# A mixture-of-experts combine: the last slot's rows by one-hot products instead of gathered rows

## The chip, the cores and the metric

The kernel runs on one core of a Trainium2 chip. The metric is the device time of one execution in microseconds (us). The engines are TensorE (PE in the profile; its weight loads are PEld), VectorE (DVE), ScalarE (ACT), GpSimd (POOL) and SyncE (SP). SP issues most DMAs; indirect DMAs are issued by POOL. Each engine works through its own queue in order.

## The reference

Four images of 384 channels by 32 x 32 (1024 tokens each) pass two layers:

```
x = x + scan_block(norm(x))                       selective scan, four directions
t = tokens(x);  t = t + moe(layernorm(t))         4 experts, 2 per token
x = x + attention(norm(x))                        8 heads of 64, q = k = v
t = tokens(x);  t = t + ffn(layernorm(t))
```

The part that matters here is `moe`: a gate gives each token a softmax over four experts, the best two are kept and their weights made to sum to one, each expert is `gelu(x @ w1 + b1) @ w2 + b2` with 384 -> 1536 -> 384, and a token's output is the weighted sum of its two experts' outputs. All is in 32-bit floats.

## The kernel before

The scan is the first loop: batch by batch, in four directions, in blocks of 128 partitions by 512 positions. POOL makes the products (L440, L468), ACT the exponentials (L449), DVE the recurrences (L454) and products (L461), PE the sums (L475). SP feeds it with loads (dtr, L424; bcs, L350). Everything behind the scan of a batch is its "tail": routing, experts, combine, attention and the feed-forward layer. The tail of batch b is written down after the scan of batch b+1, and a scheduler merges all instructions into one fixed order per engine by priorities and a model of times; the combine and some other parts have a raised priority (`high_priority(offset=FORWARD)`). So the tails of batches 0 to 2 lie among the scan's instructions, and that of batch 3 stands alone at the end.

The tail, with the names that the change touches:

- `clear` (L594) writes zeros to the array `rows` of one batch in DRAM, 19 DMAs of 128 rows on SP's queue, from a tile of zeros repeated three times per row.
- `spread` (L631) turns x to token order, stores the tokens, and normalizes them (L680). `places` (L697) computes on DVE, for each token and each of its two choices k, a row number `pos`, so that rows of one expert lie together. Then 64 indirect DMAs in all (16 per batch, L685) scatter the normalized tokens into `rows`.
- `experts` (L882) works through `rows` in NSLOT = 11 slots: eight of 256 rows, then three of 128. A slot's expert is read from a register; its weights come in eight tiles of tag "kw" (w1 in four, w2 in four), loaded by SP. `gather(s)` loads a slot's rows (tile xs) and transposes them on PE (L936) to xc. The products are h_ps (L954) and y_ps (L975); DVE adds the bias (L979), and the slot's outputs go to the array `made` in DRAM (L982; for the last slot on ACT's queue, else on SP's).
- `combine` (L986) loads the tokens, lets POOL make two diagonal matrices of gate weights (diag, L996), and then fetches the 2 x 1024 expert outputs by 16 indirect DMAs (L1005) from `made` into eight tiles got (tag "kw" as well). For each 128 tokens, `add` multiplies diag with got on PE (L1012) and adds the result to the tokens on DVE (L1015).
- `prologue` (L1024) takes the mean and variance of the new tokens (L1037, L1038), normalizes them on ACT and transposes them on PE, in two halves. `attention` (L1058) and `last_layers` (L1158) follow.

Tiles of one tag share a number of buffers: before the last batch 8 for "kw" and 5 for "k4" (slot rows, slot outputs, diag, and others); in the last batch 10 and 4. A PSUM bank of tag "p" is one of 3 in these parts.

An overflow test at the end (L518) takes the maximum of all attention sums, which are kept for all four batches.

Of the kernel before, what the change touches and what calls it, by code (L numbers as in the profile page):

```python
# [9 lines left out]
F32 = mybir.dt.float32  # L10
# [7 lines left out]
P = 128  # L18
# [25 lines left out]
NFULL = TOP * L // SLOT  # L44
NHALF = (NROW - NFULL * SLOT) // P
NSLOT = NFULL + NHALF

HEADS = 8
HD = 64
# [66 lines left out]
class Body:  # L116
# [367 lines left out]
    def open_tail(self, ctx):  # L484

        nc, tc, a = self.nc, self.tc, self.a
        self.dram = ctx.enter_context(tc.tile_pool(name="t_dram", bufs=1, space=DRAM))
        self.x2 = [
            self.dram.tile([L, D], F32, tag=f"x2_{b}", name=f"x2_{b}") for b in range(B)
        ]  # L490

        self.sums = self.const.tile(
            [P, B, HEADS // 2, MB * 2, NH], F32, tag="sums", name="sums"
        )
        return Room(tc, ctx, "t", NARROW)

    def tail_batch(self, b, x1, room):
# [7 lines left out]

    def first_layer(self, b, room):

        self.experts(b, self.slots, room)
        with self.tc.high_priority(offset=FORWARD):
            xt, xn, add = self.combine(b, *self.place, room)  # L510
            return self.prologue(xt, xn, room, add)

    def second_layer(self, b, xc, room, between):
        att = self.attention(xc, self.sums[:, b], room)
        with self.tc.high_priority(offset=FORWARD):
            self.last_layers(b, att, room, between if b < 2 else ())

    def overflow(self, room):  # L518

        nc = self.nc  # L520
        flag = self.const.tile([1, 1], I32, tag="flag", name="flag")
        top = room.tile([P, 1], "top", "top")
        nc.vector.tensor_reduce(
            top, self.sums.rearrange("p b t m i -> p (b t m i)"), AX.X, ALU.max
        )
# [21 lines left out]
    def moe_consts(self, room):  # L547
        nc, a, wp = self.nc, self.a, self.const


        turn = wp.tile([P, DC, P + NE], F32, tag="turn", name="turn")
        wg = turn[:, :, P:]
        nc.sync.dma_start(out=wg, in_=a["wg"].rearrange("(c p) e -> p c e", p=P))
        for c in range(DC):
            nc.vector.tensor_copy(turn[:, c, :P], self.ident)
        ps = room.bank("p", "wg_ps")
        for c in range(DC):
            nc.tensor.matmul(ps[:, :NE], self.ones, wg[:, c, :], start=(c == 0), stop=(c == DC - 1))
# [24 lines left out]
        self.slot_at = count("slot_at", [NSLOT], [[1, NSLOT]])  # L583


        size = NROW
        self.zero = wp.tile([P, P], F32, tag="zero", name="zero")
        nc.gpsimd.memset(self.zero, 0.0)
        self.rows, self.made = [], []
        for b in range(B):  # L590
            self.rows.append(self.dram.tile([size, D], F32, tag=f"rows{b}", name=f"rows{b}"))
            self.made.append(self.dram.tile([size, D], F32, tag=f"made{b}", name=f"made{b}"))

    def clear(self, b):  # L594

        nc = self.nc
        self.zeroed = []
        for at in range(0, NROW, P):
            ins = nc.sync.dma_start(
                out=self.rows[b][at : at + P, :].rearrange("p (c d) -> p c d", c=DC),  # L600
                in_=self.zero.unsqueeze(1).to_broadcast([P, DC, P]),
            ).ins
            self.depend(ins, self.under_way[b])
            self.zeroed.append(ins)
# [26 lines left out]
    def spread(self, b, x1, room):  # L631
# [39 lines left out]
        pos, gate, expert = self.places(sc, room)  # L671

        placed = []
        for m in range(MB):
            if m % 2 == 0:
                xt = room.tile([P, 2, D], "k4", "xt")
                nc.sync.dma_start(out=xt, in_=self.tokens(b)[:, m : m + 2, :])
            nc.scalar.activation(  # L680
                xt[:, m % 2, :], xt[:, m % 2, :], AF.Identity,
                bias=less[:, m : m + 1], scale=rstd[:, m : m + 1],
            )
# [11 lines left out]
        yield (pos, gate), (expert, placed)  # L695

    def places(self, sc, room):  # L697

# [137 lines left out]
        def later(n, before, name):  # L836
# [38 lines left out]
        weight = room.tile([P, TOP, nt], "g_weight", "g_weight")  # L875
        nc.vector.tensor_reduce(
            weight.rearrange("p k m -> p (k m)"),
            gates.rearrange("p k m e -> p (k m) e"), AX.X, ALU.add,
        )
        return pos, weight, expert  # L880

    def experts(self, b, routed, room):  # L882

# [36 lines left out]

        def gather(s):
            at, size = extent(s)
            xs = room.tile([P, size // P, D], "k4", "xs")
            queue = nc.scalar if s == 0 else nc.sync
            got = queue.dma_start(
                out=xs, in_=rows[at : at + size, :].rearrange("(t p) d -> p t d", p=P)
            ).ins
            for put in placed:
                self.depend(got, put)
            xc = room.tile([P, DC, size], "k4", "xc")  # L930
            for lo in range(0, DC, HF // size):
                ps = room.bank("p", "xc_ps").rearrange("p (r l) -> p r l", l=size)
                n = min(HF // size, DC - lo)
                for c in range(lo, lo + n):
                    for t in range(size // P):
# [4 lines left out]
                nc.vector.tensor_copy(xc[:, lo : lo + n, :], ps[:, :n, :])  # L940
            return xc

        weights, xc = fetch(0), gather(0)
        for s in range(NSLOT):
# [27 lines left out]
            for t in range(size // P):  # L972
# [9 lines left out]
            queue.dma_start(  # L982
                out=made[at : at + size, :].rearrange("(t p) d -> p t d", p=P), in_=y
            )

    def combine(self, b, pos, gate, room):  # L986


        nc = self.nc
# [12 lines left out]
        for m in range(MB):  # L1002
            got.append(room.tile([P, TOP, D], "kw", "got"))
            for k in range(TOP):
                nc.gpsimd.indirect_dma_start(  # L1005
                    out=got[m][:, k, :], out_offset=None, in_=self.made[b][:, :],
                    in_offset=bass.IndirectOffsetOnAxis(ap=pos[:, k, m : m + 1], axis=0),
                )
        def add(m):
            ps = room.bank("p", "w_ps")[:, :D]  # L1010
            for k in range(TOP):
# [513 lines left out]
```

## Time and profile before

| what | value |
|---|---|
| median of 3 runs | 4249.24 us (4240.75 to 4253.25) |
| the profiled execution | 4230.72 us; span from first to last instruction 4228.9 us |
| busy: PE, DVE, ACT, POOL | 3363 (80%), 2846 (67%), 2506 (59%), 3020 us (71%) |
| mean granted TensorE clock | 0.873 of full speed |
| DMA | 693.7 MB, 410,387 packets, of which 51,088 under 512 bytes |
| clears of `rows` | 76 DMAs of 192 KB; the median issue takes 0.636 us of SP |
| indirect DMAs | 64 scatters, 64 gathers; 0.97 and 0.95 us of POOL each |
| gathers begin at (batches 0 to 3) | 1313.7, 2267.5, 3248.8, 3932.9 us |

Times in views of the trace are from the start of the span. "Idle before" is the time an engine stood before a group, with the instruction that released it behind an arrow. A busy share is an average, so it is read by stage: until about 3400 us the scan runs with the tails of batches 0 to 2 among it; from there to the end the rest of batch 2 and all of batch 3's tail remain.

### The profile page before, as it was taken

The numbers are of one execution on the slowest core, as the hardware profiler recorded it, in microseconds if no ns is written. First come the engines' busy times: TensorE is split into PE (matmuls) and PEld (weight loads), VectorE is DVE, ScalarE is ACT, GpSimd is POOL, SyncE is SP. The second block draws the span as 40 slices with busy tenths as digits, with TensorE's granted clock in tenths as the row PEclk, the third lists the DMA queues.
The fourth block names the chain that finished last, engine by engine and source line by source line (L and its number), as shares of the span: only waits on it lengthen the run. The fifth ranks groups of instructions, "written<-read, shape, count | busy, mean of one in ns | idle before, by whom it ended". The sixth has DMA issues, their size and how long they took to land.

```text
span 4228.9 us, 45721 instructions
## 1 busy us (share of the span) xinstructions
PE 3363.3 (80%) x13308; PEld 1581.4 (37%) x13308; DVE 2846.4 (67%) x4152; ACT 2505.9 (59%) x4494; POOL 3020.1 (71%) x1471
## 2 busy tenths in 40 slices
PE   6544545489897888789996888789996899999898
PEld 2111111155553223245553223245553235566323
DVE  5999997878887878788887777888886840010101
ACT  5555555556665776666665777676664763443353
POOL 5999997898988978789899878889897840000100
PEclk8666666589998999789997999789997899999999
DMA  5454464677886535667887434658887434255200
GB/s 138 125 135 123 117 174 109 187 218 218 242 249 176 153 106 147 198 178 230 251 247 220 130 100 133 200 166 242 227 250 225 117 107 143 86 174 209 64 16 31
DMA packets 410387, 693.70 MB, mean 164 GB/s; under 512 B 51088, under 2 KB 209680, under 8 KB 410128
## 3 DMA queue, kind: packets, MB, share of 16 engines
q1 hardware_dynamic: 399728, 662.71, 54.1%
q0 software_dynamic: 8192, 25.17, 1.8%
q10 hardware_dynamic: 2208, 2.82, 0.2%
q8 instruction: 107, 1.75, 0.2%
q14 instruction: 152, 1.25, 0.1%
HBM read 569.00 MB, written 121.50 MB: 163 GB/s over the span
## 4 chain that ended last, share of the span: by engine, by line
PE 37%; DVE 22%; ACT 11%; DMA 11%; POOL 9%; issue 7%; SPq 3%; DVEq 0%; POOLq 0%; ACTq 0%
PE y_ps L975 9%; PE h_ps L954 9%; DVE da L454 8%; DVE bx L454 7%; POOL bx L440 5%; DMA dtr<-dd 4%; ACT da L449 3%; PE s_ps L1099 3%; PE acc L475 3%; DVE bx L461 3%; PE o_acc L1145 3%; POOL bx L468 2%; DMA w<-in_w 2%; SPq L424 2%; DMA bcs<-both 1%
## 5 line engine op out<-in xcount | busy, mean ns | idle before, releaser
L440 POOL TENSOR_TENSOR bx<-dtr,bcs 128x1024 f32<-128x1024 f32 x768 | 1794.0, 2363 | 201.6 <-PE acc L475 92.4
L449 ACT ACTIVATE da<-dtr,nega 128x512 f32<-128x512 f32 x1536 | 1045.3, 690 | 898.3 <-DVE bx L461 540.9
L468 POOL TENSOR_TENSOR bx<-bx,bcs 128x1024 f32<-128x1024 f32 x384 | 905.1, 2362 | 133.3 <-DVE carry L465 60.5
L475 PE MATMUL acc<-bx,sel 128*32 128x512 f32 x3072 | 500.2, 697 | 294.0 <-POOL bx L468 256.8
L954 PE MATMUL h_ps<-xc,w 128*128 128x256 f32 (+1 forms) x3168 | 675.8, 370 | 71.0 <-DMA w<-in_w 40.0
L975 PE MATMUL y_ps<-w,hs 128*128 128x384 f32 x1824 | 634.4, 500 | 26.7 <-ACT hs L967 20.1
L954 PEld LDWEIGHTS h_ps<-xc,w 128*128 128x128 f32 x3168 | 561.0, 201 | 240.7 <-issue 120.2
L454 DVE TENSOR_TENSOR_SCAN bx<-da,carry,bx 128x512 f32<-128x512 f32 x384 | 473.5, 1270 | 112.9 <-ACT da L449 57.7
L454 DVE TENSOR_TENSOR_SCAN da<-da,carry,bx 128x512 f32<-128x512 f32 x384 | 477.3, 1275 | 60.9 <-ACT da L449 50.2
L454 DVE TENSOR_TENSOR_SCAN bx<-da,bx 128x512 f32<-128x512 f32 x384 | 453.5, 1211 | 90.4 <-ACT da L449 56.8
L461 DVE TENSOR_TENSOR bx<-da,bcs 128x512 f32<-128x512 f32 x768 | 511.0, 681 | 4.0
L454 DVE TENSOR_TENSOR_SCAN da<-da,bx 128x512 f32<-128x512 f32 x384 | 456.1, 1219 | 76.6 <-ACT da L449 64.8
L975 PEld LDWEIGHTS y_ps<-w,hs 128*128 128x128 f32 x1824 | 348.4, 195 | 306.2 <-issue 64.7
L1105 ACT ACTIVATE ex<-s_ps 128x512 f32<-128x512 f32 x512 | 300.8, 592 | 130.1 <-PE s_ps L1099 126.6
L1099 PE MATMUL s_ps<-w 64*128 64x512 f32 x1024 | 310.6, 664 | 61.6 <-ACT ex L1105 56.3
L962 ACT ACTIVATE hs<-h_ps,bb 128x256 f32<-128x256 f32 (+1 forms) x528 | 200.5, 441 | 212.4 <-PE h_ps L954 208.2
L996 POOL TENSOR_TENSOR diag<-ident,g_weight 128x1024 f32<-128x1024 f32 x8 | 15.0, 1896 | 424.3 <-PE xc_ps L936 410.6
L1145 PE MATMUL o_acc<-ex,vt 128*64 128x512 f32 x1024 | 284.7, 633 | 24.0 <-ACT ex L1105 16.8
L475 PEld LDWEIGHTS acc<-bx,sel 128*32 128x32 f32 x3072 | 75.8, 116 | 594.1 <-POOL bx L468 361.7
L979 DVE TENSOR_TENSOR y<-y_ps,bb 128x384 f32<-128x384 f32 x76 | 41.6, 547 | 230.9 <-PE y_ps L975 230.6
L1099 PEld LDWEIGHTS s_ps<-w 64*128 64x128 f32 x1024 | 83.8, 190 | 267.2 <-ACT ex L1105 219.0
L365 PE MATMUL dt_ps<-xd,wdt 108*128 108x512 f32 x192 | 123.1, 728 | 63.4 <-ACT mag L404 34.4
(222 smaller groups left out, 3613.0 us busy)
## 6 DMA issues: line engine op xcount, KB each, us to landing
w<-in_w SPq DMA_DIRECT2D x352, 576.0 KB
dtr<-dd SPq DMA_DIRECT2D x1536, 128.0 KB
bcs<-both SPq DMA_DIRECT2D x512, 128.0 KB
dd<-one_e SPq DMA_DIRECT2D x96, 256.0 KB
dd<-mag SPq DMA_DIRECT2D x96, 256.0 KB
rows<-zero SPq DMA_DIRECT2D x76, 192.0 KB
xt<-x SPq DMA_DIRECT2D x32, 384.0 KB
made<-y SPq DMA_DIRECT2D x32, 384.0 KB
```

Of the source, the lines that this page charges most:

```text
L440: pool = nc.gpsimd.tensor_mul(bx, dtr[q][1], bc[:, 0].unsqueeze(1).to_broadcast([P, 2, HF])).ins
L449: nc.scalar.activation(da, dtr[q][0][:, j, :], AF.Exp, scale=nega[:, col : col + 1])
L454: nc.vector.tensor_tensor_scan(run(h), run(da), run(bx[:, j, :]), 0.0 if first else hold, ALU.mult, ALU.add,)
L461: dve = nc.vector.tensor_mul(bx[:, j, :], h, cg).ins
L468: pool = nc.gpsimd.tensor_mul(bx, bx, cg.unsqueeze(1).to_broadcast([P, 2, HF])).ins
L475: nc.tensor.matmul(acc[lo : lo + DB, :], sel, out[q][:, j, :], start=(g == 0), stop=(g == NG - 1),)
L954: ins = nc.tensor.matmul(ps[:, r, :], w1[(f + r) // wf][:, c, (f + r) % wf * P : ((f + r) % wf + 1) * P], xc[:, c, :], start=(c == 0), sto ...
L962: done = nc.scalar.activation(hs[:, f + r, :], ps[:, r, :], AF.Gelu if last else AF.Identity, bias=bb[:, f + r : f + r + 1],).ins
L975: nc.tensor.matmul(out[:, :D], hs[:, f, t * P : (t + 1) * P], w2[f // wf][:, f % wf, :], start=(f == 0), stop=(f == FC - 1),)
L1099: ins = nc.tensor.matmul(ps, w[rows, j * P : (j + 1) * P], w[rows, halves(i)], start=True, stop=True).ins
L1105: done.append(nc.scalar.activation(ex[:, o, :], ps, AF.Exp, scale=HD**-0.5, accum_out=sums[:, t, 2 * j + o, i : i + 1],).ins)
L1145: ins = nc.tensor.matmul(out[cols, :], made[t][1][:, j, cols], ex[:, o, :], start=(j == 0), stop=(j == MB - 1),).ins
```

## The change

The last slot's outputs are no longer stored and gathered. Each row in `rows` is one number wider (W = D + 1 = 385) and carries its token's number, 1 to 1024 (0 in a cleared row). When the last slot's rows are loaded, DVE compares that number with the numbers of each group of 128 tokens and gets eight one-hot matrices (`own`, tag "k4"). In `combine`, PE multiplies each with the last slot's output y (in SBUF), and DVE adds the product, times the gate weight `near` of tokens that have a row there, to the tokens. The gathers read `made` without its last 128 rows: where a token's row is in the last slot, its gather reads row 0 and its weight is 0. The rows are cleared by DMAs in pieces of 77 numbers, the largest divisor of 385 up to 128. The attention sums get a tile per batch instead of one for all, and each batch leaves one column of maxima.

```diff
+STORED = NROW - P
+W = D + 1
+WC = max(w for w in range(1, P + 1) if W % w == 0)
...
+        self.number = count("number", [MB], [[P, MB]], base=1, channel=1)
+        self.column = count("column", [P], [[1, P]], base=1)
...
@@ clear
-                out=self.rows[b][at : at + P, :].rearrange("p (c d) -> p c d", c=DC),
-                in_=self.zero.unsqueeze(1).to_broadcast([P, DC, P]),
+                out=self.rows[b][at : at + P, :].rearrange("p (c d) -> p c d", d=WC),
+                in_=self.zero[:, :WC].unsqueeze(1).to_broadcast([P, W // WC, WC]),
...
@@ spread
-                xt = room.tile([P, 2, D], "k4", "xt")
-                nc.sync.dma_start(out=xt, in_=self.tokens(b)[:, m : m + 2, :])
+                xt = room.tile([P, 2, W], "k4", "xt")
+                nc.sync.dma_start(out=xt[:, :, :D], in_=self.tokens(b)[:, m : m + 2, :])
+                nc.scalar.copy(xt[:, :, D:], self.number[:, m : m + 2].unsqueeze(2))
...
@@ places
+        nc.vector.tensor_scalar(stored, place, float(STORED) - 0.5, None, op0=ALU.is_lt)
+        nc.vector.tensor_mul(place, place, stored)
+        nc.vector.tensor_copy(source, place)
+        nc.vector.tensor_mul(weight, both, stored)
+        nc.vector.tensor_sub(rest, both, weight)
+        nc.vector.tensor_reduce(near, rest.rearrange("p k m -> p m k"), AX.X, ALU.add)
...
@@ experts, gather(s)
+            if s == NSLOT - 1:
+                apart = room.tile([P, MB], "apart", "apart")
+                nc.vector.tensor_sub(apart, xs[:, 0, D:].to_broadcast([P, MB]), self.full)
+                own = room.tile([P, MB, P], "k4", "own")
+                for m in range(MB):
+                    nc.vector.tensor_scalar(
+                        own[:, m, :], self.column, apart[:, m : m + 1], None, op0=ALU.is_equal
+                    )
...
-            queue = nc.sync if s + 1 < NSLOT else nc.scalar
-            queue.dma_start(
-                out=made[at : at + size, :].rearrange("(t p) d -> p t d", p=P), in_=y
-            )
+            if s + 1 < NSLOT:
+                nc.sync.dma_start(
+                    out=made[at : at + size, :].rearrange("(t p) d -> p t d", p=P), in_=y
+                )
...
@@ combine, behind the 16 gathers
+        own, y = last
+        for m in range(MB):
+            ps = room.bank("p", "n_ps")[:, :D]
+            nc.tensor.matmul(ps, own[:, m, :], y[:, 0, :], start=True, stop=True)
+            nc.vector.scalar_tensor_tensor(
+                xt[:, m, :], ps, near[:, m : m + 1], xt[:, m, :], op0=ALU.mult, op1=ALU.add
+            )
...
@@ second_layer
+        sums = room.tile([P, HEADS // 2, MB * 2, NH], "sums", "sums")
+        att = self.attention(xc, sums, room)
+        nc.vector.tensor_reduce(
+            self.tops[:, b : b + 1], sums.rearrange("p t m i -> p (t m i)"), AX.X, ALU.max
+        )
```

More of the change, by code (lines that the diff above doesn't have):

```diff
@@ L490, in open_tail @@
         ]
-        self.sums = self.const.tile(
-            [P, B, HEADS // 2, MB * 2, NH], F32, tag="sums", name="sums"
-        )
+        self.tops = self.const.tile([P, B], F32, tag="tops", name="tops")
         return Room(tc, ctx, "t", NARROW)
@@ L506, in first_layer @@
     def first_layer(self, b, room):
-        self.experts(b, self.slots, room)
+        last = self.experts(b, self.slots, room)
         with self.tc.high_priority(offset=FORWARD):
-            xt, xn, add = self.combine(b, *self.place, room)
+            xt, xn, add = self.combine(b, *self.place, last, room)
             return self.prologue(xt, xn, room, add)
     def second_layer(self, b, xc, room, between):
-        att = self.attention(xc, self.sums[:, b], room)
+        sums = room.tile([P, HEADS // 2, MB * 2, NH], "sums", "sums")
+        att = self.attention(xc, sums, room)
+        nc = self.nc
+        nc.vector.tensor_reduce(
+            self.tops[:, b : b + 1], sums.rearrange("p t m i -> p (t m i)"), AX.X, ALU.max
+        )
         with self.tc.high_priority(offset=FORWARD):
@@ L522, in overflow @@
         top = room.tile([P, 1], "top", "top")
-        nc.vector.tensor_reduce(
-            top, self.sums.rearrange("p b t m i -> p (b t m i)"), AX.X, ALU.max
-        )
+        nc.vector.tensor_reduce(top, self.tops, AX.X, ALU.max)
         ps = room.bank("p", "top_ps")
@@ L590, in moe_consts @@
         for b in range(B):
-            self.rows.append(self.dram.tile([size, D], F32, tag=f"rows{b}", name=f"rows{b}"))
-            self.made.append(self.dram.tile([size, D], F32, tag=f"made{b}", name=f"made{b}"))
+            self.rows.append(self.dram.tile([size, W], F32, tag=f"rows{b}", name=f"rows{b}"))
+            self.made.append(self.dram.tile([STORED, D], F32, tag=f"made{b}", name=f"made{b}"))
     def clear(self, b):
@@ L670, in spread @@
         less = self.less_mean(mv[:, :, 0], rstd, room, "r_less")
-        pos, gate, expert = self.places(sc, room)
+        pos, expert, place = self.places(sc, room)
         placed = []
@@ L677, in spread @@
             if m % 2 == 0:
-                xt = room.tile([P, 2, D], "k4", "xt")
-                nc.sync.dma_start(out=xt, in_=self.tokens(b)[:, m : m + 2, :])
+                xt = room.tile([P, 2, W], "k4", "xt")
+                nc.sync.dma_start(out=xt[:, :, :D], in_=self.tokens(b)[:, m : m + 2, :])
+                nc.scalar.copy(xt[:, :, D:], self.number[:, m : m + 2].unsqueeze(2))
             nc.scalar.activation(
-                xt[:, m % 2, :], xt[:, m % 2, :], AF.Identity,
+                xt[:, m % 2, :D], xt[:, m % 2, :D], AF.Identity,
                 bias=less[:, m : m + 1], scale=rstd[:, m : m + 1],
@@ L694, in spread @@
                 placed.append(put)
-        yield (pos, gate), (expert, placed)
+        yield place, (expert, placed)
     def places(self, sc, room):
@@ L874, in places @@
         nc.vector.tensor_mul(gates, chosen, sc.unsqueeze(1).to_broadcast([P, TOP, nt, NE]))
-        weight = room.tile([P, TOP, nt], "g_weight", "g_weight")
+        both = small([P, TOP, nt])
         nc.vector.tensor_reduce(
-            weight.rearrange("p k m -> p (k m)"),
+            both.rearrange("p k m -> p (k m)"),
             gates.rearrange("p k m e -> p (k m) e"), AX.X, ALU.add,
         )
-        return pos, weight, expert
+        stored = room.tile([P, TOP, nt], "g_stored", "g_stored")
+        nc.vector.tensor_scalar(stored, place, float(STORED) - 0.5, None, op0=ALU.is_lt)
+        nc.vector.tensor_mul(place, place, stored)
+        source = room.sb.tile([P, TOP, nt], I32, tag="g_source", name="g_source", bufs=2)
+        nc.vector.tensor_copy(source, place)
+        weight = room.tile([P, TOP, nt], "g_weight", "g_weight")
+        nc.vector.tensor_mul(weight, both, stored)
+        rest = room.tile([P, TOP, nt], "g_rest", "g_rest")
+        nc.vector.tensor_sub(rest, both, weight)
+        near = room.tile([P, nt], "g_near", "g_near")
+        nc.vector.tensor_reduce(near, rest.rearrange("p k m -> p m k"), AX.X, ALU.add)
+        return pos, expert, (source, weight, near)
     def experts(self, b, routed, room):
@@ L922, in gather @@
             at, size = extent(s)
-            xs = room.tile([P, size // P, D], "k4", "xs")
+            xs = room.tile([P, size // P, W], "k4", "xs")
             queue = nc.scalar if s == 0 else nc.sync
@@ L940, in gather @@
                 nc.vector.tensor_copy(xc[:, lo : lo + n, :], ps[:, :n, :])
+            if s == NSLOT - 1:
[6 more added lines that the diff above has]
+                    )
+                self.own = own
             return xc
@@ L979, in experts, with combine @@
                 nc.vector.tensor_add(y[:, t, :], out[:, :D], bb[:, FC:])
-            queue = nc.sync if s + 1 < NSLOT else nc.scalar
-            queue.dma_start(
-                out=made[at : at + size, :].rearrange("(t p) d -> p t d", p=P), in_=y
-            )
-    def combine(self, b, pos, gate, room):
+            if s + 1 < NSLOT:
+                nc.sync.dma_start(
+                    out=made[at : at + size, :].rearrange("(t p) d -> p t d", p=P), in_=y
+                )
+        return self.own, y
+    def combine(self, b, pos, gate, near, last, room):
         nc = self.nc
```

## The prediction

> **What bounds the kernel now.** I read four views, in this order. First the page's slices of the span (one digit is the busy share of 105.7 us in tenths):
>
> ```profile
> PE   6544545489897888789996888789996899999898
> ...
> POOL 5999997898988978789899878889897840000100
> ```
>
> POOL is nearly full until slice 31; after it PE is full to the end. So the scan (on POOL, DVE and ACT) sets the time to about 3400 us and TensorE sets the rest, with the tail of batches 0 to 2 threaded through the scan. Second, the timeline around the last batch's combine (start, length, engine, then in brackets how long the engine had been idle and who released it):
>
> ```profile
> 3921.61 8.01 PE L975 MATMUL y_ps<-w,hs 128*128 128x384 f32 x24 [2.04 <-ACT hs L959]
> ...
> 3930.25 0.34 ACTq L982 DMA_DIRECT2D made<-y  x1
> 3932.91 1.01 POOL L1005 DMA_INDIRECT got<-made,g_pos  x1 [12.44 <-DMA made<-y]
> 3935.97 0.97 POOL L1005 DMA_INDIRECT got<-made,g_pos  x1 [2.06 <-issue]
> ...
> 3936.21 1.62 PE L1012 MATMUL w_ps<-got,diag 128*128 128x384 f32 x2 [6.59 <-DMA got<-made,g_pos]
> ```
>
> Here nothing else runs: the last slot's product ends at 3929.6, is stored, and only then do 16 gathers go out, 1.256 us apart. Third, busy time by stage around the same place in batch 1 (columns: length; PE, PEld, DVE, ACT, POOL busy; granted clock; DMA share; GB/s):
>
> ```profile
> 2235.00:2257.00 22.00, 19.96 (x114) 13.77 (x114) 14.48 (x16) 16.95 (x29) 19.65 (x11) 0.94 0.77 244
> 2257.00:2268.00 11.00, 2.14 (x11) 0.35 (x9) 10.86 (x13) 7.50 (x13) 10.85 (x6) 0.70 0.39 125
> 2268.00:2288.00 20.00, 14.94 (x46) 6.91 (x47) 6.28 (x15) 6.02 (x12) 15.42 (x17) 0.67 0.73 214
> 2288.00:2310.00 22.00, 7.79 (x27) 3.35 (x25) 18.86 (x30) 8.83 (x16) 20.29 (x10) 0.66 0.57 143
> ```
>
> PE is idle for 28 of the 53 us after the product (2257 to 2310), and in the 20 us of the gathers DVE and ACT stand at 30%, for POOL issues gathers and feeds them nothing. Fourth, the chain of waits where SP clears the next batch's rows:
>
> ```profile
> 3205.71 12.58 DMA rows<-zero
> ...
> 3224.49 0.64 SPq L599
> ...
> 3225.18 0.63 SPq L599
> ...
> 3230.12 3.61 DMA dtr<-dd
> ```
>
> The clear stands on the chain, and the scan's own loads (dtr) are queued behind it.
>
> **Part 1, the exposed combine of batch 3.** Before: the product ends at 3929.6 and the statistics of the first half of the tokens are done at 3948.98 (ACT's first instruction after them). After, the gathers no longer wait for the last slot's store. They need the store of the slot before (issued 3915.96; POOL is released by it at 3918.57) and diag (done 3920.5). With 2 us before the second (the 2.06 above) and 1.256 each, the eighth goes out at about 3931.3 and lands 3.2 later (median of the gathers), 3934.5. What is added lies on the path: eight one-hot products of two passes each. The nearest row is the slot's own product, 24 passes in 7.74 us, so 0.645 for one, 5.2 for eight. They run 3930.3 to 3935.5, and DVE's eight multiply-adds (0.552 each, from L1015, same shape, one bank) keep pace. Then four w_ps of 1.29 (the pace of L1015 in the second half, 3955.66 to 3959.53) end at 3940.7, and the last add, statistics and aggregate are 1.3: about 3942. That is 7 earlier; with the clock of 0.73 granted there (3930 to 3955; 0.97 in the 150 us before) the ten us of products become up to 14 and 3 remain. I take **-6**. Bounds: -12, the whole shift of the gathers (3932.9 to 3920.5), if the products hid too; +5 if the second diag came last (rival D). What is late next is TensorE itself: from here it is busy to the end.
>
> **Part 2, the same in batches 0 to 2.** TensorE's 5.2 us of one-hot products have cover: it is idle for 15 us in 1290 to 1334, 28 in 2257 to 2310 and 22 in 3208 to 3254. Without that cover they would cost 5.2 each. The 64 gathers stay (rows that are not stored read row 0), so POOL's 20.1 us per batch stay too, and the scan stands still for them wherever they are. What can be won is that they lie beside the last slot's products (8.0 to 10.9 us on PE) rather than behind them. Ends: 0, since POOL's sum is the same, and -20, if all of the block moves beside work. I take batch 3's figure, -6 each, for it is the same chain: **-18**.
>
> **Part 3, the rows are one number wider.** 385 elements have 77 as their largest divisor up to 128, so each of the 19 clears of a batch writes 640 pieces of 308 bytes where it wrote 384 of 512. Now 19 clears take 12.86 us (1414), 13.33 (2314), and 14.4 for 17 of them at 3211, at a DMA share of 0.86 to 1.07. Ends: by bytes nothing; by pieces 640/384 x 0.64 us, so 0.43 more each and 8.2 per batch; and 4.6 per batch below nothing if SP's issue alone decided (wqkv, a load of 384 pieces of 512 bytes, is issued in 0.40). The engines are full in these stretches, so I take the pieces. The chain passes right behind the clears at 534 (POOL then waits 0.42 us for dtr), through those at 2314 and 3205, and not through that at 1414: three of four, **+24.6**. The DMA page of the Trainium skill ("DMA: Bandwidth & Descriptors", Specifications) speaks against this part: it says that transfers below 512 bytes miss line rate because the engine reads, modifies and writes. If by that rule the bytes cost twice, a clear would be 1.28 us, an estimate, and this term 36 in place of 24.6. The profile counts 51,088 packets under 512 bytes, but no large transfer of this kernel is made of them, so no row shows their price.
>
> **Part 4, VectorE and ScalarE.** Per batch DVE gains eight comparisons for the one-hot (128x128; between 0.19 for 128x32 at L737 and 0.414 for 128x384 at L1175, so about 0.25, 2.0 together), the eight multiply-adds (4.4) and seven small ones (0.17, 1.2): 7.6. In the slices of the combines DVE is 72 to 76% busy, and it is what hides them; without cover it would be 7.6 per batch. I take 1 for each of three batches, **+3**. The comparisons run before the last slot's product ends, with only that batch's scan behind them. The extra place arithmetic comes after the positions are cast, so the scatter does not wait for it in data. ACT's 16 copies of a number (0.17, as L541) are hidden behind the scatters' 1.27 us pace. The maxima of the sums (0.68 at 4132, long before the end) become four smaller ones, nothing. The scatter's 64 issues of 0.97 stay; one float more per row is nothing to them. The last slot's store leaves ACT's queue (0.34), nothing.
>
> **Sum**: -6 - 18 + 24.6 + 3 = +3.6 on the profiled execution, 4230.7 to 4234.3. That execution lies 18.5 below the median of the three runs (4249.2), so I carry the difference: 4253.
>
> **The rivals.** About 0.3%, 12.7 us, is what can be told from no change.
>
> *A, the forecast*: the terms cancel, 4240 to 4266.
>
> *B, the clears cost by bytes and the gathers lie well*: part 3 nothing, half of the 20.1 us beside the products in each batch: -6 - 30 + 3 = -33, **4216**. For it: PE's 15 to 28 idle us; DMA is only at 0.86 in two clears. Against: DMA at 1.07 in the last.
>
> *C, a new wait on POOL, slower*: the tiles that the gathers fill share eight buffers with the expert weights. In batches 0 to 2 the last slot's weights fill all eight: the first eight gathers wait for its h_ps products, the other eight for its y_ps products. A gather that waits in POOL's queue holds the scan's multiplications behind it, and DVE and ACT behind those. It decides once the y_ps product ends later than 17.6 us (14 gathers) after POOL reached the first. Price: the 12.4 us that POOL stood at its first gather in batch 3, with nothing behind; here three times with the scan behind: -6 + 36 + 24.6 + 3 = +58, **4307**. For it: POOL's queue is in order and 90% full. Against: in batches 0 to 2 it now waits at most 1.26 us at gathers.
>
> *D, it does not do what it says*: the tag k4 has four buffers in batch 3, and the one-hot holds one until its last product. If the second diag gets that one, it starts at 3935.5, ends at 3937.4, and the gathers, if queued behind it, begin 4.5 us later than now, and the statistics with them. With nothing won in the other batches: +5 + 24.6 + 3 = +33, **4282**. For it: in batch 3 the second diag already waits for a buffer, until 3918.57. Against: two other buffers come free before the one-hot's.
>
> **How the numbers follow.** A 0.36, B 0.30, C 0.18, D 0.16. A's upper end is past 4262, so 0.06 of it counts as slower: faster 0.30, same 0.30, slower 0.06 + 0.18 + 0.16 = 0.40. The range reaches from B to between D and C: 4213 to 4296; outside are the better half of B's spread (0.10) and C's worse half (0.09). A's own range is 4240 to 4266.
>
> **What would show it.** Part 1: the first gather of batch 3 starts before the last y_ps product ends, and the first half's statistics end 12 to 16 us behind that product, where it is 19.4 now. Part 2: no gather behind the last slot's product in batches 0 to 2, and the PE idle time there shrinks. Part 3: SP's 19 clears take 21 us (13 if bytes decide), and data packets under 512 bytes rise by 48,640. C would show as POOL waiting for PE at a gather; D as a diag released by a one-hot product. I am wrong if the order in which the engines' queues are written changes elsewhere too: any shift in the scan of more than 13 us outweighs all of this.

## The result and the profile after

| | before | after |
|---|---|---|
| median of 6 runs each | 4242.66 us (4240.75 to 4253.25) | 4359.54 us (4350.44 to 4365.40) |
| ratio, 95% interval | | 1.0267 (1.0252 to 1.0283) |
| span of the profiled execution | 4228.9 us | 4348.6 us |
| POOL idle behind dtr loads (line of the first scan product) | 80.1 us | 180.3 us |
| packets; under 512 bytes | 410,387; 51,088 | 429,268; 99,664 |
| the scan's last product on POOL ends at | 3412.9 us | 3516.5 us |
| from there to the end of the span | 816.0 us | 832.1 us |

The change costs 113 us by the ratio and 120 by the two profiled spans. The last two rows say where: 104 us are lost while the scan runs, 16 behind it. The slices of the span (a slice is now 108.7 us) show the same; POOL loses tenths in many slices of the scan, and still ends in slice 32:

```profile
PE   6445434489887688789987688879985799999899
...
POOL 5999977898888677879889768889885840000100
```

The largest loss is found by looking for what POOL waits for. This is the timeline of the changed kernel where SP clears batch 1's rows (start, length, engine, line, operation; in brackets the idle time before and who ended it), SP's queue first (the view opens behind the first of the 19 clears), then POOL:

```profile
1431.78 32.36 SPq L605 DMA_DIRECT2D rows<-zero  x18
1464.24 4.00 SPq L353 DMA_DIRECT2D bcs<-both  x4
1469.56 5.83 SPq L427 DMA_DIRECT2D dtr<-dd  x4
```

```profile
1445.66 2.36 POOL L471 TENSOR_TENSOR bx<-bx,bcs 128x1024 f32<-128x1024 f32 x1 [3.04 <-DVE carry L468]
1477.70 13.89 POOL L443 TENSOR_TENSOR bx<-dtr,bcs 128x1024 f32<-128x1024 f32 x6 [29.68 <-DMA dtr<-dd]
```

In the kernel before, the same clear on SP's queue was this line:

```profile
1413.94 12.86 SPq L599 DMA_DIRECT2D rows<-zero  x19
```

The clears now hold SP's queue for 33 us, the scan's loads stand behind them, and POOL stops for 29.7 us. It stops in the same way at all four clears: 25.3, 29.7, 22.8 and 27.0 us, **104.8 together**. SP's 19 issues of one clear took 12.9 to 13.3 us before (19.3 in batch 3, in two groups); they take 32.0, 33.0, 34.2 and 36.7 now. SP is held because the DMA engines are: here are 15 us from the first issue of batch 0's clear, where little else is under way. The columns are the window and its length, busy time of PE, PEld, DVE, ACT and POOL, the granted clock, the DMA share and GB/s. The kernel before:

```profile
534.07:549.07 15.00, 3.87 (x16) 0.40 (x16) 14.30 (x16) 6.67 (x10) 15.00 (x7) 0.51 0.86 259
```

The changed kernel, with the 15 us that follow:

```profile
529.78:544.78 15.00, 3.87 (x16) 0.40 (x16) 14.30 (x16) 6.67 (x10) 15.00 (x7) 0.50 1.24 105
544.78:559.78 15.00, 3.87 (x16) 0.40 (x16) 7.90 (x10) 4.07 (x6) 7.44 (x4) 0.50 1.38 100
```

The DMA engines are busier than before (1.24 to 1.38 against 0.86) and move 40% as much. More pieces alone, at the old price of a piece, would have left 384/640, 60%; so each piece takes longer as well.

Behind the scan, look first at the combine of batch 3, the one whose working the prediction shows. The timeline of the changed kernel (the lines between, 14 gathers among them, are left out):

```profile
4039.69 0.98 POOL L1035 DMA_INDIRECT got<-made,g_source  x1 [440.26 <-issue]
...
4042.32 8.01 PE L1004 MATMUL y_ps<-w,hs 128*128 128x384 f32 x24 [2.04 <-ACT hs L988]
...
4050.98 5.43 PE L1042 MATMUL n_ps<-y,own 128*128 128x384 f32 x16 [0.65 <-DVE y L1008]
...
4060.30 0.94 POOL L1035 DMA_INDIRECT got<-made,g_source  x1 [0.30 <-issue]
4061.26 3.76 POOL L1026 TENSOR_TENSOR diag<-ident,g_weight 128x1024 f32<-128x1024 f32 x2
...
4063.23 7.74 PE L1050 MATMUL w_ps<-got,diag 128*128 128x384 f32 x16 [6.82 <-POOL diag L1026]
...
4072.79 0.30 ACT L155 ACTIVATE rstd<-mv,eps 128x4 f32<-128x4 f32 x1 [28.18 <-DVE mv L1076]
```

The second diag and the first statistics in the kernel before:

```profile
3918.57 1.89 POOL L996 TENSOR_TENSOR diag<-ident,g_weight 128x1024 f32<-128x1024 f32 x1 [13.73 <-DMA made<-y]
...
3948.98 0.30 ACT L152 ACTIVATE rstd<-mv,eps 128x4 f32<-128x4 f32 x1 [25.09 <-DVE mv L1038]
```

The gathers do start 10.6 us before the last product ends (4050.3), and the one-hot products take 5.43 us. But the two diag products, which in the kernel before stood ahead of the gathers on POOL, now stand **behind all sixteen**, PE waits 6.82 us for them, and the first statistics are ready 22.5 us behind the product, where it was 19.4.

That gain is missed, but the 16 us lost behind the scan do not lie here: from the last product to the end of the span it is 298.3 us, against 299.3 before. They lie in front of it, between the scan's last product and the last product of batch 3's experts, where PE is busy for 495 of 517 us before and 511 of 534 now. What is left of batch 2's attention is worked off there. These views of that stretch count the products of attention scores (s_ps) alone, all of them of batch 2 (columns: busy time of PE, PEld, ACT with counts; clock, DMA share, GB/s). The kernel before, then the changed one:

```profile
3412.90:3929.60 516.70, 44.75 (x150) 11.91 (x148) 48.27 (x152) 0.98 0.44 149
```

```profile
3516.50:4050.30 533.80, 54.09 (x180) 14.50 (x180) 57.65 (x182) 0.97 0.44 147
```

Of a batch's 256 score products 180 are left when the scan ends, where it was 150, and the stretch is 17 us longer.

### The profile page after: what moved, and what is told of

It is laid out like the page before. It is cut to its first block, busy times and chain, and to the rows that moved or that the text cites. A ratio compares the mean times of both kernels' runs of the same rounds, so it can differ in the third digit from the quotient of the medians.

```text
span 4348.6 us, 45959 instructions
## 1 busy us (share of the span) xinstructions
PE 3377.8 (78%) x13372; PEld 1592.3 (37%) x13372; DVE 2870.9 (66%) x4250; ACT 2511.3 (58%) x4512; POOL 3020.7 (69%) x1473
## 2 busy tenths in 40 slices
DMA packets 429268, 693.04 MB, mean 159 GB/s; under 512 B 99664, under 2 KB 228560, under 8 KB 429008
## 3 DMA queue, kind: packets, MB, share of 16 engines
q14 instruction: 153, 1.25, 0.1%
## 5 line engine op out<-in xcount | busy, mean ns | idle before, releaser
L443 POOL TENSOR_TENSOR bx<-dtr,bcs 128x1024 f32<-128x1024 f32 x768 | 1794.3, 2366 | 287.2 <-DMA dtr<-dd 180.3
L1004 PE MATMUL y_ps<-w,hs 128*128 128x384 f32 x1824 | 644.5, 507 | 71.6 <-ACT hs L996 35.6
L1035 POOL DMA_INDIRECT got<-made,g_source x64 | 61.0, 953 | 460.3 <-issue 454.2
```

Of the source, the lines that this page charges most:

```text
L443: pool = nc.gpsimd.tensor_mul(bx, dtr[q][1], bc[:, 0].unsqueeze(1).to_broadcast([P, 2, HF])).ins
L1004: nc.tensor.matmul(out[:, :D], hs[:, f, t * P : (t + 1) * P], w2[f // wf][:, f % wf, :], start=(f == 0), stop=(f == FC - 1),)
```

## The experiments

Ratios are to runs of the kernel before that were taken on the same chip beside the kernel in question: 4272.09 us for experiments 1 to 4, 4247.64 for 5 and 7 to 9, 4248.79 for 6 and 10 to 12. Times of different chips are compared by these ratios. "Whole" below means that a piece starts and ends on a multiple of 32 bytes of the array, "cut" that it does not.

**Theories.** *Short pieces*: the clear in 308-byte pieces costs nearly all of it, because pieces under 512 bytes are dear. *Cut ends*: 308 is no multiple of the block that memory is written in, and that is what costs, not the length. *The rest*: the wider rows, the one-hot work or the order of the queues.

**1. The changed kernel, one piece of 1540 bytes a row.**

```diff
-                out=self.rows[b][at : at + P, :].rearrange("p (c d) -> p c d", d=WC),
-                in_=self.zero[:, :WC].unsqueeze(1).to_broadcast([P, W // WC, WC]),
+                out=self.rows[b][at : at + P, :],
+                in_=self.zero,
```

> The changed kernel, but each row is cleared in one piece of 1540 bytes (from a wider tile of zeros) instead of five of 308. Theory 1 (short pieces make the clears slow and the scan's loads wait behind them on SP): a batch's 19 clears fall from 32 to 37 us to 13 or less, the four waits of POOL for dtr behind them (25, 30, 23, 27 us) vanish, and the time falls by about 100, to 4245 to 4265. Theory 1b (it is not the length but the start off a 64-byte line, as the row pitch is 1540 bytes): clears stay above 25 us and the time above 4320. Theory 2 (gathers among the scan's products and the one-hot products hold up the scan): clears fall, but the time stays above 4310.

Measured: 4298.17 us, ratio 1.0061 (1.0038 to 1.0084). Of 2.67%, 2.1 are gone with the pieces alone: some 87 us, where about 100 was foretold. The clears of batches 0 to 2 took SP 10.7 to 12.0 us. So a start off the line does not by itself make a piece slow (theory 1b), for most rows of 1540 bytes start off it too; with short pieces it does, as run 3 shows.

**2. The kernel before, with the changed kernel's clear and nothing else.** The array is 385 numbers a row long and cleared whole in 308-byte pieces; rows stay 384 wide.

```diff
-                out=self.rows[b][at : at + P, :].rearrange("p (c d) -> p c d", c=DC),
-                in_=self.zero.unsqueeze(1).to_broadcast([P, DC, P]),
+                out=self.flat[b][at * W : (at + P) * W].rearrange("(p c d) -> p c d", p=P, d=WC),
+                in_=self.zero[:, :WC].unsqueeze(1).to_broadcast([P, W // WC, WC]),
```

> The kernel before, with nothing changed but the clears: the array has room for 385 numbers per row and is cleared whole in pieces of 308 bytes, 640 per DMA; rows themselves stay 384 wide. Theory 1: 19 clears take 32 to 37 us and the time rises by 80 to 115 over the kernel before, nearly all of the change's loss. Theory 2: it rises by less than 40.

Measured: 4382.94 us, ratio 1.0259 (1.0242 to 1.0276). The clear alone makes the loss: 111 us, with clears of 35.7 to 39.7 us on SP. In the page's group of the scan's first product the wait for dtr is 161.5 us (180.3 in the changed kernel, 80.1 in the kernel before):

```profile
L442 POOL TENSOR_TENSOR bx<-dtr,bcs 128x1024 f32<-128x1024 f32 x768 | 1792.5, 2360 | 296.7 <-DMA dtr<-dd 161.5
```

**3. Length against position.** The kernel before, each batch's clear in another kind of piece: 384 bytes, 256 bytes, 512 bytes moved by 4, 768 bytes.

```diff
+PIECE = (96, 64, 128, 192)
+SHIFT = (0, 0, 1, 0)
...
+                out=self.flat[b][SHIFT[b] + at * D : SHIFT[b] + (at + P) * D].rearrange(
+                    "(p c d) -> p c d", p=P, d=PIECE[b]
+                ),
```

> The kernel before as a probe: batch 0 clears its rows in pieces of 384 bytes, batch 1 in 256, batch 2 in 512 shifted by 4 bytes, batch 3 in 768. Read are the times of SP's 19 clears. If a piece has a fixed price when short (48 ns per engine, as the changed kernel's 1.94 us for 640 pieces gives): 1.55 us each for 384 bytes, 2.3 for 256. If the bytes count double below 512: 1.3 for both. If pieces cost the same as those of 512 bytes (27 ns): 0.85 and 1.28. The shifted ones stay at 0.64 if only length counts, and go above 1.2 if a start off the line has its own price; 768 bytes: 0.65 or less.

Measured: 4307.59 us (one run). The windows of 15 us from the first issue of batches 0 (384), 1 (256) and 2 (512 moved by 4), columns as above:

```profile
531.80:546.80 15.00, 3.87 (x16) 0.41 (x16) 14.30 (x16) 6.67 (x10) 15.00 (x7) 0.50 0.93 258
```

```profile
1421.97:1436.97 15.00, 11.37 (x58) 4.36 (x57) 14.77 (x27) 11.24 (x25) 13.08 (x7) 0.77 1.15 263
```

```profile
2337.58:2352.58 15.00, 13.28 (x51) 6.29 (x52) 12.72 (x13) 9.99 (x18) 8.92 (x5) 0.70 1.17 124
2352.58:2367.58 15.00, 5.90 (x26) 1.45 (x20) 3.12 (x5) 7.09 (x14) 3.20 (x2) 0.87 1.28 115
```

SP's 19 issues took 13.3, 13.4 and 23.1 us, so 0.70, 0.70 and 1.21 each. For the first two that is below the least that was foretold (0.85 and 1.28). Position decides. Pieces of 384 and even 256 bytes run at 258 and 263 GB/s, as the 512-byte pieces of the kernel before; pieces of **512 bytes that start 4 bytes off** run at 124. Length alone is refuted.

**4. The changed kernel, cleared flat in whole 512-byte pieces.**

```diff
+        flat = self.rows[b].rearrange("r d -> (r d)")
...
+                out=flat[lo : lo + step].rearrange("(p c d) -> p c d", p=P, d=P),
+                in_=self.zero.unsqueeze(1).to_broadcast([P, DC, P]),
```

> The changed kernel, its array cleared as one run of numbers in pieces of 512 bytes on 512-byte boundaries, as the kernel before does it (one more small DMA per batch for the rest). Theory 1 and 1b: clears of 13 us, time 4240 to 4265, the same as with one piece of 1540 bytes under theory 1, and 60 or more faster than it under 1b. What is left against the kernel before is the one-hot and the order of the queues: my sum without part 3 gave -21, theory 2 gives more than +60.

Measured: 4285.56 us, ratio 1.0036 (1.0021 to 1.0051). It cannot be told from run 1, and it lies between what my sum without part 3 gave (-21 us) and what theory 2 asked for (over +60): some 15 us of loss. Without the cut pieces the change is still not a gain; something else eats what parts 1 and 2 should bring.

**5. How large is the block.** As 3: batch 0 in 512-byte pieces moved by 64 bytes, batch 1 by 32, batch 2 by 16, batch 3 in 768-byte pieces moved by 4.

```diff
-PIECE = (96, 64, 128, 192)
-SHIFT = (0, 0, 1, 0)
+PIECE = (128, 128, 128, 192)
+SHIFT = (16, 8, 4, 1)
```

> The kernel before, its clear in pieces whose start is shifted by a constant: batch 0 in 512-byte pieces shifted by 64 bytes, batch 1 by 32 bytes, batch 2 by 16 bytes, batch 3 in 768-byte pieces shifted by 4 bytes. Theory "cut ends" (a piece whose ends do not fall on a block boundary costs more, whatever its length; 512-byte pieces shifted by 4 bytes took a DMA share of 1.29 at 118 GB/s, while 384 and 256 bytes unshifted took 0.94 to 1.09 at 257 to 271 GB/s): batch 0 about 13 us and 250 GB/s if blocks are 64 bytes, batch 1 the same only if blocks are 32 bytes, batch 2 slow in both cases, batch 3 slow but per byte about two thirds of the extra of a shifted 512-byte piece. Slow is a stretch of at least 20 us with a DMA share over 1.15 at under 160 GB/s. Theory "length" (only pieces under 512 bytes are dear): all four batches at 240 GB/s or more.

Measured: 4269.27 us (one run). Batches 0, 1 and 2:

```profile
529.55:544.55 15.00, 3.87 (x16) 0.40 (x16) 14.30 (x16) 6.67 (x10) 15.00 (x7) 0.50 1.07 252
```

```profile
1415.80:1430.80 15.00, 11.37 (x57) 4.44 (x56) 14.77 (x27) 11.25 (x25) 13.34 (x7) 0.77 1.09 261
```

```profile
2320.00:2335.00 15.00, 8.95 (x32) 3.39 (x30) 13.42 (x24) 11.54 (x22) 15.00 (x8) 0.97 1.16 122
```

Moved by 64 and by 32 bytes a piece runs at 252 and 261 GB/s, moved by 16 at 122. Of the moves tried, those by whole 32-byte blocks cost little (a mean of 34 ns for 27 in the trace's records of single pieces), and a piece that cuts a block is dear. Batch 3 lay among other loads (SP's issues took 26 us), and its rate could not be read.

**6. What a cut piece costs.** As 3, all moved by 4 bytes, in pieces of 768, 256, 384 and 512 bytes.

```diff
+PIECE = (192, 64, 96, 128)
+SHIFT = (1, 1, 1, 1)
```

> The kernel before, its clears shifted by 4 bytes in all batches, in pieces of 768, 256, 384 and 512 bytes. Measure: DMA-engine time in the 80 us from the first issue of the clear, where unshifted pieces took 49 to 55 us in batch 0, 37 to 45 in batch 1, 38 to 49 in batch 2. Theory "a price for each cut piece", 40 to 64 ns on its engine: 256 bytes (912 pieces an engine) take 36 us more or fill the 80 us, 384 bytes (608) 24 to 39 us more, 768 bytes (304) 12 to 19 us more. Rival "long pieces hide it": 768 bytes take at most 5 us more, as pieces of 1540 bytes did (49.6), and below some length each piece takes a fixed time whatever it carries. Under "length alone" 768 and 512 bytes would take nothing more.

Measured: 4389.36 us (one run). Batches 0 (768), 1 (256) and 2 (384); batch 3 again lay among other loads:

```profile
531.10:546.10 15.00, 3.87 (x16) 0.40 (x16) 14.30 (x16) 6.67 (x10) 15.00 (x7) 0.51 1.06 166
```

```profile
1425.60:1440.60 15.00, 11.37 (x59) 4.56 (x58) 14.77 (x28) 11.40 (x25) 13.49 (x6) 0.77 1.40 78
```

```profile
2370.70:2385.70 15.00, 11.81 (x50) 5.43 (x50) 12.81 (x13) 10.01 (x17) 10.93 (x6) 0.87 1.20 101
```

In time per piece on one of 16 engines (16 x bytes / rate; an estimate, since the windows hold a little other traffic), and behind it the mean of the pieces' own durations, of which the trace has one record each:

| piece, bytes | whole: GB/s, ns, mean record | cut: GB/s, ns, mean record |
|---|---|---|
| 256 | 263, 16, 18 | 78, 53, 95 |
| 308 | | 105, 47, 66 |
| 320 (run 7) | 229, 22, 26 | |
| 384 | 258, 24, 22 | 101, 61, 85 |
| 512 | 259, 32, 27 | 124, 66, 79 |
| 768 | record 36 (run 3, batch 3) | 166, 74, 88 |
| 1540 (run 1) | | 261, 94, 98 |

Whole pieces take time about by their bytes, down to 256. By the rate a cut piece takes 47 to 74 ns up to 768 bytes, and at 1540 the rate is that of whole 512-byte pieces. The records show more than the rates. Some cut pieces are as short as whole ones (20 ns for a quarter of those of 308 bytes), others take several times as long, and the mean lies 32 to 77 ns above the short ones, at 1540 bytes too (98 against 66; in the kernel before, half of all whole 1536-byte packets take 65 or less). So long pieces pay as well; it does not push their rate below that of whole 512-byte pieces. Neither of the simple forms on record holds, not by bytes and not one fixed addition. The engine time in the 80 us from the first issue was 57.3 us for the 768-byte pieces (50.2 in the kernel before), 7 more with 1.6 MB less of all traffic done, where the first form asked for 12 to 19; for 384 bytes it was about 39 more (24 to 39 foretold), and those of 256 bytes filled the 80 us, as foretold. One thing is not told apart: in every cut clear here a block that one piece cuts is also written by its neighbour, so the price may be that of a block written in part or of a block that two pieces share.

**7. The changed kernel with rows of 1600 bytes, cleared in pieces of 320.** The number stands 16 times in each row.

```diff
-W = D + 1
-WC = max(w for w in range(1, P + 1) if W % w == 0)
+W = D + 16
+WC = 80
```

> The changed kernel with rows of 400 values (1600 bytes; the token number stands 16 times in each) and the clear in pieces of 320 bytes, five a row, 640 a DMA for each engine's sixteenth 40, nothing else changed. Theory "cut ends": 320 bytes are a multiple of 64, so a clear costs as the aligned ones, 12 to 17 us a batch and 220 to 280 GB/s, and the ratio is 1.000 to 1.006. Theory "length": 320 bytes are as dear as 308, about 30 to 36 us a batch at 100 to 120 GB/s, ratio 1.022 to 1.030.

Measured: 4276.66 us, ratio 1.0063 (1.0038 to 1.0088), a hair above what cut ends had foretold (1.000 to 1.006) and far from the 1.022 of short pieces; SP's clears of batches 0 to 2 took 14.6 to 15.8 us. In the same place as above:

```profile
532.90:547.90 15.00, 3.87 (x16) 0.41 (x16) 14.30 (x15) 6.67 (x10) 15.00 (x8) 0.50 1.15 229
```

Twelve bytes more a piece, and the rate is 229 for 105.

**8. Wide rows alone.** The kernel before with rows of 385 numbers scattered and loaded, cleared as in 4; no one-hot products.

```diff
-                xt = room.tile([P, 2, D], "k4", "xt")
+                xt = room.tile([P, 2, W], "k4", "xt")
...
-            xs = room.tile([P, size // P, D], "k4", "xs")
+            xs = room.tile([P, size // P, W], "k4", "xs")
```

> The kernel before with rows of 385 values (1540 bytes) scattered and loaded, the clear in aligned 512-byte pieces, no one-hot products: combine, made and gathers as in the kernel before. Theory "wide rows": rows that start off a block cost their scatter and their loads, and the 0.36 percent that stays with aligned pieces comes from them: ratio 1.002 to 1.006. Rival "the rest": the scatter is off the chain and rows of 1540 bytes cost nothing, ratio 0.998 to 1.002, and the 0.36 percent lies with the one-hot products, the added vector work or the order of the program.

Measured: 4243.38 us, ratio 0.9992 (0.9977 to 1.0006). No cost of rows of 1540 bytes is seen in scatter and load.

**9. Gathers behind the diags.** The kernel of 4, the 16 gathers put behind the second diag on POOL, as the kernel before had them.

```diff
+                with self.tc.issue_after(formed.ins):
                     nc.gpsimd.indirect_dma_start(
```

> The changed kernel with the clear in aligned 512-byte pieces, and the 16 gathers of a combine put behind its two diag products on GpSimd. Theory "order on GpSimd": in batch 3 the two diags no longer stand behind 16 gathers that are ready early, w_ps follows the one-hot products at once, the first rstd comes 12 to 16 us behind the last y_ps product (22.5 in the changed kernel, 19.4 in the kernel before), and the time falls 4 to 8 us below the 1.0036 of the kernel with aligned pieces, so a ratio of 1.002 to 1.003. Rival "made up for later": the first half of batch 3's layer starts earlier but the second half waits for the same thing as before, the time from the last y_ps product to the end stays at 298 to 300 us, ratio 1.003 to 1.005.

Measured: 4235.12 us, ratio **0.9982** (0.9967 to 0.9996): the lowest ratio of all, a little below the kernel before and below both foretold ranges (1.002 to 1.003, and 1.003 to 1.005 for the rival). The timeline of batch 3's combine, to lay beside that of the changed kernel:

```profile
3929.36 3.75 POOL L1036 TENSOR_TENSOR diag<-ident,g_weight 128x1024 f32<-128x1024 f32 x2 [387.01 <-DMA made<-y]
3933.00 8.01 PE L1014 MATMUL y_ps<-w,hs 128*128 128x384 f32 x24 [2.04 <-ACT hs L998]
3933.25 1.01 POOL L1046 DMA_INDIRECT got<-made,g_source  x1 [0.15 <-POOL diag L1036]
...
3941.65 5.43 PE L1053 MATMUL n_ps<-y,own 128*128 128x384 f32 x16 [0.65 <-DVE y L1018]
...
3946.92 5.32 PE L1061 MATMUL w_ps<-got,diag 128*128 128x384 f32 x16
...
3953.68 0.30 ACT L155 ACTIVATE rstd<-mv,eps 128x4 f32<-128x4 f32 x1 [18.40 <-DVE mv L1087]
```

The w_ps products follow the one-hot products with no gap, and the statistics are ready 12.7 us behind the last product (3941.0). From that product to the end of the span it is 291.9 us; 299.3 before, 298.3 after. But the whole step from 4 is 0.54%, 23 us, three times what batch 3 can give by its earlier statistics (19.7 us behind the product in 4, 12.7 here).

**10 and 11. Which batches the order matters in.** The kernel of 9 with the order in batch 3 only, and in batches 0 to 2 only.

```diff
+                with self.tc.issue_after(formed.ins) if b == B - 1 else nullcontext():
```

> The changed kernel with aligned 512-byte pieces; the gathers stand behind the diag products on GpSimd in batch 3 only, batches 0 to 2 are free as in the changed kernel. With the order in all batches the ratio was 0.9982, with none 1.0036. Theory "the order of batches 0 to 2 takes most": batch 3 alone gives the 7 us by which its first rstd comes earlier (12.7 us behind the last y_ps product against 19.7), ratio 1.001 to 1.003. Rival "batch 3 is all of it": ratio 0.997 to 1.000.

> The counterpart: the gathers stand behind the diags in batches 0 to 2 and are free in batch 3. Theory "the order of batches 0 to 2 takes most": ratio 0.999 to 1.001, first rstd of batch 3 still 19 to 23 us behind the last y_ps product. Rival "batch 3 is all of it": ratio 1.002 to 1.005.

Measured: batch 3 only 1.0042 (1.0022 to 1.0062), batches 0 to 2 only 1.0008 (0.9993 to 1.0023). The first theory holds for the second figure and misses with the first, which shows no gain over the 1.0036 of run 4 at all. The rival is out on the first, and on the second but for the end of the interval. The statistics of batch 3 came as foretold, 12.7 us behind the product with the order and 22.4 without it (19 to 23 foretold). By these ratios the order of batches 0 to 2 gives 0.28 points alone and 0.60 beside that of batch 3. That of batch 3 gives nothing alone and 0.26 beside the others, which is hardly more than the intervals.

How batches 0 to 2 gain is seen in what is left when the scan ends. These windows are those of the result section, from the scan's last product to batch 3's last y_ps product, with the score products alone. The kernels of 4 and of 9:

```profile
3443.20:3985.90 542.70, 55.17 (x176) 14.43 (x176) 56.29 (x178) 0.97 0.44 145
```

```profile
3457.90:3941.00 483.10, 30.59 (x96) 8.01 (x96) 30.77 (x98) 0.98 0.48 161
```

The same for experiments 10 (batch 3 only) and 11 (batches 0 to 2 only), which ran on one chip:

```profile
3432.80:3975.40 542.60, 54.68 (x176) 14.16 (x176) 56.31 (x178) 0.97 0.43 144
```

```profile
3467.70:3956.30 488.60, 28.85 (x96) 7.66 (x96) 30.80 (x98) 0.97 0.47 160
```

Without the order in batches 0 to 2, 176 of a batch's 256 score products are left, with it 96, and the stretch, which PE fills, is 54 to 60 us shorter. Part of that is given back, for the scan ends later, by 35 us between 10 and 11. (Between 4 and 9 it is 15, but there the chips differ.) The order put POOL's gathers elsewhere, and the scheduler then wrote more of batch 2's attention beside the scan. Which of its choices did that is not shown: the written order of PE differs between the two kernels all along from batch 0's combine.

**12. The changed kernel with the order alone**, its cut pieces left.

```diff
+                with self.tc.issue_after(formed.ins):
                     nc.gpsimd.indirect_dma_start(
```

> The changed kernel, its clear in 308-byte pieces left as it is, with the gathers behind the diags in all batches. Theory "two separate causes": the order gives about the 0.54 percent that it gave beside aligned pieces, 1.0267 - 0.0054 = 1.021 (1.018 to 1.024). Rival "one hides the other": GpSimd stands behind the clear anyway, the order gives nothing but the 7 us of batch 3, ratio 1.024 to 1.027.

Measured: 4316.50 us, ratio 1.0174 (1.0145 to 1.0204). The order gives 0.93 points here (39 us) beside the cut pieces, so neither cause hides the other; the value lies just below the foretold range and its interval reaches into it. In the profile the scan ends where it did (3517.7; 3516.5 in the changed kernel), and the rest is 796.7 us in place of 832.1, with 124 score products left in place of 180.

## Why the prediction was wrong, point by point

Forecast 4253 us, measured 4359.54, outside the range of 4213 to 4296. Against the kernel before that is +3.6 us said and +113 measured by the ratio. Of the 110 between, 73 to 86 are the price of part 3; the rest is the gain of parts 1 and 2, which the order of the queues took (23 to 39 us, runs 9 and 12).

**Part 3 failed.** The step was "by pieces 640/384 x 0.64 us, so 0.43 more each and 8.2 per batch", +24.6 in all. It scaled the clear with the number of pieces at the old price of a piece. A 308-byte piece does not take the 32 ns of a whole 512-byte piece but 47, so a clear of 19 took 32 to 37 us and not 21. POOL's four waits behind the clears are 104.8 us; by removal the term is 2.31% (run 4 against the changed kernel, 98 us), and added to the kernel before it is 2.59% (run 2, 110 us). It was also 4 of 4 clears on the chain, not 3. Both ends that I gave for it, 4.6 a batch below nothing and 8.2 above, were too low: I had bounded a piece's price from rows that held only whole pieces. The packets under 512 bytes rose by 48,576, where I had counted 48,640: there are 48,640 pieces of 308 bytes, and 64 fewer packets of 4 bytes. The count was right and said nothing of the price.

The page that I weighed against this part ("DMA: Bandwidth & Descriptors" of the Trainium skill, Specifications) led to an estimate of 36, nearer but also too low. It draws the line at 512 bytes, which the runs do not bear out, for whole pieces of 256, 320 and 384 bytes ran at 229 to 263 GB/s and 512-byte pieces that cut a block at 122 to 124. Whether the engine reads, modifies and writes for a cut piece, no run shows. The same page (How a descriptor splits into AXI transactions) gives an AXI beat as 32 bytes, which is the block that run 5 points to; that the beat is the cause, no run here shows.

**Part 1 was right in its terms and wrong in one order.** The gathers moved ahead of the product's end, the one-hot products took 5.43 (5.2 said; the view's 8.01 us for 24 passes, where I put 7.74, gives 5.3), DVE's eight multiply-adds 5.07 (4.4 said). But "diag (done 3920.5)" was taken as standing first in POOL's queue. Once the gathers no longer waited for the last store, the scheduler wrote them ahead of both diags. By which of its rules is not shown: in run 9 diag is released by the store of the slot before the last (made<-y), the one that the gathers need as well. With the old order (run 9) the statistics came 12.7 us behind the product, at the near end of the 12 to 16 foretold, and from product to end it is 7.4 us less than before, where the changed kernel has 1.0 less: the -6 was there, and the queue's order took it. Rival D named the late diag, but for another reason: the one-hot's buffer. In run 9 the one-hot holds the same buffer and the diags are done before the last product ends, so the buffer need not have held them up.

**Part 2 was the wrong end of its range.** The combines of batches 0 to 2 did get shorter. In run 9 the first statistics came 20.3, 22.3 and 21.2 us behind the last slot's product, where it was 29.8, 24.6 and 48.8 before. PE's idle time in the 50 us behind the product fell as foretold, from 22, 28 and 27 us to 17, 20 and 21 in the changed kernel, but that is little more than the one-hot products' own 5.4. Yet run 9 as a whole is 0.18% (7.6 us) below the kernel before, and batch 3 alone has 7.4 less behind its product. So of the -18 nothing is left in the sum; it is the end "0, since POOL's sum is the same" that fits, with the added work of part 4 in the same sum. The check that I gave, no gather behind the product, was not met either: 8, 9 and 16 of 16 gathers went out behind it in the changed kernel. What I had left out is the other side of a changed order: how much of a batch's attention the scheduler writes beside the scan (150, 180 or 96 score products left, at 54 to 60 us for 80 of them).

**Part 4** cannot be told apart in time. DVE's added work is 24.5 us for four batches (2870.9 - 2846.4), 6.1 each where I had 7.6, and run 9 carries it and is still not slower than the kernel before; no run takes it away alone.

**The rivals.** C is excluded: in batches 0 to 2 of the changed kernel POOL stood at no gather for more than 0.5 us (the gathers of batch 0 went out 1.25 us apart). B's first half, clears by bytes, holds for whole pieces and only for those. The last sentence of the prediction, that a changed order elsewhere can outweigh all, came true in size: the order of POOL's gathers moved the time by 23 to 39 us, as much as the 24 that parts 1 and 2 were to bring, or more.

Not settled: which single choice of the written order in batches 0 to 2 leaves more of batch 2's attention behind the scan. The gap between run 4 (1.0036) and the kernel before is closed by the order, and wide rows are not in it (run 8).

## What to carry to other kernels

When a row gets wider, look at what the new width does to the pieces of every bulk DMA that uses it: keep starts and lengths at multiples of 32 bytes (pad the row, or clear the array flat), or make cut pieces long, as the 1540 bytes of run 1. Price a new kind of transfer by a row of its own kind; where the profile has none, its upper bound is not the price of the nearest whole piece. And when a wait is taken away, look at which instruction is now written first on that queue, and tie the order down where another engine waits for the second.

## What the runs showed of the hardware that was not expected

- A write to DRAM in pieces that cut a 32-byte block ran at 78 to 124 GB/s for 256 to 512 bytes, against 229 to 263 for pieces that do not. By these rates a cut piece keeps an engine 47 to 66 ns; at 1540 bytes the rate is 261.
- Meanwhile the DMA share of the profile stands at 1.16 to 1.40 in those windows. A high share at a falling rate was the mark of it; whole pieces stood at 0.86 to 1.15, so the share alone does not tell.
- Scatter and load of rows of 1540 bytes showed no cost against 1536 (ratio 0.9992, 0.9977 to 1.0006).
